# Attention, Strassen projections and a Winograd convolution on one core: softmax sums of eight heads in the first batch, stores on SP's queue, two prepared weight parts moved, and a transform ahead of outputs

## The chip, the cores and the metric

The kernel runs on one core of a Trainium2 chip. The core has a matrix engine (TensorE, PE in the profile, with its weight loads as PEld), a vector engine (VectorE, DVE), a scalar engine (ScalarE, ACT), GpSimd (POOL) and SyncE (SP). Each executes its own instructions in order and waits on semaphores for the others. SP and POOL also issue DMAs: a DMA instruction stands in its engine's order like any other, so one that waits holds back what is queued behind it. The metric is the device time of one execution in microseconds (us); the median of four runs is given. The profile is one more execution.

## What is computed

`x` is (4, 1024, 32, 32). Layer 0 is attention over the 1024 positions of each image: with 1024 channels as 16 heads of 64,

```
qkv = x @ w_qkv.T + b_qkv
q, k = rmsnorm(rope(q)), rmsnorm(rope(k))
attn = softmax(q @ k.T * 64**-0.5)
out  = rmsnorm((attn @ v) @ w_proj.T) + x
```

Layer 1 is a bottleneck block: 1x1 convolution to 256 channels, 3x3 convolution, 1x1 convolution back to 1024, each with a batch norm over the whole batch; ReLU after the first two, and after the residual sum at the end. All is float32.

## The kernel before

**Stages.** The four images ("batches" b = 0 to 3) go one after the other through the projections of q, k and v, attention, and the output projection y. Then come conv1, conv2 and conv3, all of them with activations that stay on the core or are read back from HBM.

**Projections.** Each 1024 x 1024 product is a Strassen-Winograd product (7 products of half-size blocks in place of 8). `project` does one level; it is used for q and k of batch 0. `project2` (L459) does two levels, 49 products. Sums of weight blocks are prepared once, in batch 0, and kept in HBM: `wd` holds first-level sums, `wd2` second-level ones. `prepare` (L385) makes the four sums of one outer part: four loads of 256 KB, four DVE operations of 128 x 512 (`make`, L391), four stores of 256 KB into `wd2` (L397). `prepare_blocks` (L401) does the same for `wd`. In both the stores are issued by POOL. Weight tiles come from a ring of eight buffers (`wring`), and the pieces that are prepared during attention use the same ring.

**The order of the work** is written by hand for PE, POOL, DVE and ACT: each runs its instructions in the order of the Python calls. SP's order is left to the framework. Within the projections a step can be put off by a number of products (`after(n, step)`); one product is some 3.43 us of PE time. `weight_parts` (L1122) queues loads on POOL at a given product and `make` some products later. Rotations of q and k (`turn`, L717) are queued items, run as a budget of DVE time allows.

**Attention.** `attention` (L767) runs for two halves (c = 0, 1) of the queries; each half has eight head pairs. This document counts them 0 to 15 through a batch. For a pair, 16 score products (L787, each shown as two instructions) go through ACT's exponential (L794) into eight tiles `p`; DVE adds the eight tiles into `den` (L798, L800); PE multiplies `p` with v (L808). The eight `p` tiles have no second copy. The sum of `den` over its 128 partitions is a PE product with a matrix of ones. It is done in one of two ways:

- *By pairs* (L837 to L843, `fold` is None): after every odd pair, PE sums the `den` tiles of two pairs at once, four products that show as eight instructions `dn` (L841). `inverses` (L885) then copies the result, stores it in `dens`, loads it back over all partitions, and two steps later DVE takes the reciprocal (L899), and `spread` (L905) loads it back to both halves of a tile by eight loads on SP for each two pairs.
- *By eights* (`fold` is two tiles of `T0` and `T2`): `halve` (L848) adds a pair's lower and upper 64 partitions with accumulating DMAs on POOL, so that two pairs share one tile. After four pairs, and two pairs late, `sum_of_eight` (L857) sums all four with four products (L861, eight instructions), and one pair after that the reciprocal (L868) and 16 `spread` loads follow.

Either way `mean_of_v` (L761), after odd pairs, multiplies the result by the spread reciprocals (DVE L764, POOL L765). Before the change only c = 0 of batches 1 to 3 goes by eights. In batch 0 attention also prepares 21 weight parts (`todo`, L1204): `load_parts` (L1210) loads at most two ahead with SP, and `make` runs after the pairs, one or two at a time, all done by pair 14.

**conv2** is a Winograd convolution. For each batch four items (f, h) follow each other, 2 x 2 of 128 output channels and row halves. An item's products are `uv` (L1418): a first half, then ACT copies both PSUM banks out (`copies`, L1432, into the ring `tmp` of four tiles, two for an item), then a second half into the same banks. `outputs` (L1442) combines banks and copies on DVE (L1445, L1446, and more when h is 1). It runs for the item before the current one. `steps` holds the next batch's input transform, 16 DVE operations (L1357), four of which run after each item's outputs. The last four write the tile `V` that the next batch's first item reads.

The order of one item, L1501 to L1518:

```python
uv(b, f, h, 0, 1)
copies(b, f, h)
...
for i in range(NPT):
    uv(b, f, h, 1, i)
if due:
    outputs(*due)
due = (b, f, h)
for step in steps[:4]:
    step()
steps = steps[4:]
```

Of the kernel before, what the change touches and what calls it, by code (L numbers as in the profile page):

```python
# [18 lines left out]
P = 128  # L19
# [66 lines left out]
def program(ctx, tc, x, wblk, w2, w3, vecs, cos, sin, out, bad):  # L86
# [71 lines left out]
    with tc.tile_pool(name=f"st{u}", bufs=2) as st, ExitStack() as s:  # L158
# [226 lines left out]
        def prepare(which, base, k, alloc, queue):  # L385
# [15 lines left out]
        def prepare_blocks(base, g, alloc, queue):  # L401
# [6 lines left out]
            def make():  # L408
# [4 lines left out]
                for o, t in enumerate((a11, a22, a21, a12)):  # L413
                    nc.gpsimd.dma_start(wd[base // NT * NG + g, o], t)
# [707 lines left out]
        def weight_parts(parts, first, step, lag, alloc):  # L1122

            for i, part in enumerate(parts):
                after(first + i * step, lambda part=part: after(lag, part(alloc, nc.gpsimd)))

        def pieces_of(tile, cols=NCH):
# [3 lines left out]
            def alloc(name):  # L1131
# [8 lines left out]
                lambda alloc, queue, which=which, base=base, k=k: prepare(which, base, k, alloc, queue)  # L1140
# [5 lines left out]
        def blocks_of(base):  # L1146
            return [lambda alloc, queue, g=g: prepare_blocks(base, g, alloc, queue) for g in range(NG)]
# [16 lines left out]
        for b in range(B):  # L1164
# [8 lines left out]
            if b == 0:  # L1173
                unused = kp.tile([P, NT, N], F32, tag="k", name="unused")
                parts = [
                    lambda alloc, queue, g=g: prepare_blocks(WV, g, stay(room, g), queue) for g in range(NG)
                ]
# [9 lines left out]
            if b == 0:  # L1187
# [3 lines left out]
                weight_parts([parts_of[WQ][0]], 14, 0, 4, pieces_of(room[:, : NT // 2, :]))  # L1191
# [301 lines left out]
        for b in range(B):  # L1493
# [8 lines left out]
            for f in range(NPT):  # L1502
                for h in range(2):
# [153 lines left out]
```

## Time and profile before

| | us |
|---|---|
| median of 4 runs (lowest, highest) | 2673.92 (2672.91, 2675.62) |
| the profiled execution, its own time | 2674.97 |
| span of its trace | 2672.7 |
| PE busy | 2644.0 (99%) |
| DVE busy | 2112.4 (79%) |
| ACT busy | 1111.9 (42%) |
| POOL busy | 472.2 (18%) |
| batch 0: k projection, from, to | 104.7, 201.7 |
| batch 0: attention, from, to | 287.7, 522.2 |
| batch 1: q projection, from, to | 609.7, 696.3 |
| conv2, from, to | 2432.4, 2547.0 |

The stages are read from the first and last PE instruction of their tiles; times of places count from the start of the span. In rows of the timeline the columns are: start, duration of the merged group, engine, line, operation, tiles written and read, shapes, count, and in brackets the idle time before the group and what ended it. The granted TensorE clock is at full speed through all 40 slices of the profile.

### The profile page before, as it was taken

The numbers are of one execution on the slowest core, as the hardware profiler recorded it, in microseconds if no ns is written. First come the engines' busy times: TensorE is split into PE (matmuls) and PEld (weight loads), VectorE is DVE, ScalarE is ACT, GpSimd is POOL, SyncE is SP. The second block draws the span as 40 slices with busy tenths as digits, with TensorE's granted clock in tenths as the row PEclk, the third lists the DMA queues.
The fourth block names the chain that finished last, engine by engine and source line by source line (L and its number), as shares of the span: only waits on it lengthen the run. The fifth ranks groups of instructions, "written<-read, shape, count | busy, mean of one in ns | idle before, by whom it ended". The sixth has DMA issues, their size and how long they took to land. (4 is left out here: it accounts for less than half of the span.)

```text
span 2672.7 us, 32558 instructions
## 1 busy us (share of the span) xinstructions
PE 2644.0 (99%) x11338; PEld 1651.0 (62%) x11338; DVE 2112.4 (79%) x2538; ACT 1111.9 (42%) x1549; POOL 472.2 (18%) x573
## 2 busy tenths in 40 slices
PE   9999999999999999999999999999999999999997
PEld 4448533488888333688886333888884335846843
DVE  5678899988787866788878667887988679877987
ACT  2222455423442655433343655233425654312266
POOL 2542234301001221200111222100111222010000
PEclk9999999999999999999999999999999999999999
DMA  7887676767567451456775531665774443583165
GB/s 272 292 257 216 198 243 207 234 210 247 170 182 213 81 103 46 154 152 223 190 194 148 95 74 36 209 202 178 192 213 87 83 99 112 172 278 106 64 235 207
DMA packets 255627, 459.22 MB, mean 172 GB/s; under 512 B 34912, under 2 KB 127632, under 8 KB 255456
## 3 DMA queue, kind: packets, MB, share of 16 engines
q1 hardware_dynamic: 210528, 306.73, 36.5%
q0 software_dynamic: 44928, 150.33, 22.3%
q8 instruction: 93, 1.52, 0.2%
q14 instruction: 78, 0.64, 0.1%
HBM read 327.43 MB, written 97.01 MB: 159 GB/s over the span
## 5 line engine op out<-in xcount | busy, mean ns | idle before, releaser
L794 ACT ACTIVATE p<-sc 128x1024 f32<-128x1024 f32 x512 | 476.3, 1043 | 26.4 <-PE sc L787 24.8
L787 PE MATMUL sc<-q,k 64*128 64x512 f32 x2048 | 457.7, 596 | 0.0
L800 DVE TENSOR_TENSOR den<-den,p 128x1024 f32<-128x1024 f32 x312 | 384.9, 1234 | 33.6 <-DVE den L800 1.4
L787 PEld LDWEIGHTS sc<-q,k 64*128 64x128 f32 x2048 | 189.9, 186 | 265.2 <-issue 121.6
L808 PE MATMUL cx<-p,to 128*64 128x512 f32 x1536 | 340.2, 595 | 0.0
L808 PEld LDWEIGHTS cx<-p,to 128*64 128x64 f32 x1536 | 106.0, 137 | 228.7 <-issue 228.7
L480 PE MATMUL p_v<-w_v,x 128*128 128x256 f32 x928 | 210.0, 379 | 2.1 <-DVE x L451 2.1
L485 PE MATMUL p_y<-q,w_y 128*128 128x256 f32 x928 | 209.8, 379 | 0.0
L765 POOL TENSOR_SCALAR q<-q,vec 128x512 f32<-128x512 f32 x64 | 129.0, 2023 | 384.5 <-DVE q L764 376.3
L480 PEld LDWEIGHTS p_v<-w_v,x 128*128 128x128 f32 x928 | 176.1, 190 | 27.4 <-DVE x L451 3.1
L485 PEld LDWEIGHTS p_y<-q,w_y 128*128 128x128 f32 x928 | 176.0, 190 | 27.1 <-issue 3.4
L813 ACT COPY q<-cx 128x512 f32<-128x512 f32 x64 | 37.6, 587 | 360.0 <-PE cx L808 360.0
L798 DVE TENSOR_TENSOR den<-p 128x1024 f32<-128x1024 f32 x52 | 64.7, 1243 | 120.3 <-ACT p L794 120.3
L485 PE MATMUL p_q<-to,w_q 128*128 128x256 f32 x672 | 152.2, 379 | 0.0
L485 PE MATMUL p_k<-to,w_k 128*128 128x256 f32 x672 | 152.2, 379 | 0.0
L485 PEld LDWEIGHTS p_q<-to,w_q 128*128 128x128 f32 x672 | 127.4, 190 | 18.4 <-issue 1.2
L485 PEld LDWEIGHTS p_k<-to,w_k 128*128 128x128 f32 x672 | 127.4, 190 | 18.4 <-issue 1.2
L808 PE MATMUL cx<-p,rq 128*64 128x512 f32 x512 | 113.4, 595 | 0.0
L1561 PE MATMUL c<-h,w 128*128 128x512 f32 x256 | 110.3, 592 | 0.5 <-ACT h L1464 0.5
L800 DVE TENSOR_TENSOR den_T<-den_T,p 128x1024 f32<-128x1024 f32 x72 | 88.2, 1225 | 7.5
L485 PE MATMUL p_y<-to,w_y 128*128 128x256 f32 x384 | 90.4, 380 | 1.7 <-DMA w_y<-wdf 1.7
L727 POOL DMA_DIRECT2D k<-ks x64 | 57.9, 1096 | 192.8 <-ACT p L794 71.1
(490 smaller groups left out, 4267.8 us busy)
## 6 DMA issues: line engine op xcount, KB each, us to landing
w_v<-wd2f SPq DMA_DIRECT2D x112, 256.0 KB, 3.5
w_y<-wd2f SPq DMA_DIRECT2D x112, 256.0 KB, 2.7
w_q<-wd2f SPq DMA_DIRECT2D x84, 256.0 KB, 2.8
w_k<-wd2f SPq DMA_DIRECT2D x84, 256.0 KB, 2.7
wd2f<-w_pre POOLq DMA_DIRECT2D x68, 256.0 KB, 4.0
x<-in_x_dram SPq DMA_DIRECT2D x64, 256.0 KB, 5.7
q<-qs POOLq DMA_DIRECT2D x64, 256.0 KB, 5.5
k<-ks POOLq DMA_DIRECT2D x64, 256.0 KB, 4.4
```

Source lines behind the costliest of these rows:

```text
L480: nc.tensor.matmul(o[:, q].rearrange("p (g f) -> p g f", g=2), r[:, i, q * P : (q + 1) * P], wt[:, :, i, :], skip_group_check=True, **at,)
L485: nc.tensor.matmul(o[:, q], wt[:, q, i, :], r[:, i, :], skip_group_check=True, **at)
L727: nc.gpsimd.dma_start(dst[i::2, f, :], other[1 - i :: 2, :], accum_op=ALU.add)
L765: nc.gpsimd.tensor_scalar(cx, cx, col("bv", hp), None, ALU.add)
L787: nc.tensor.matmul(sc[:, j], k_all[d, hp, t * P : (t + 1) * P], q_all[d, hp, at], start=True, stop=bad is not None,)
L794: nc.scalar.activation(p, sc, AF.Exp)
L798: nc.vector.tensor_tensor(d_, probs[0], p, ALU.add)
L800: nc.vector.tensor_tensor(d_, d_, p, ALU.add)
L808: nc.tensor.matmul(o[j * HD : (j + 1) * HD, :], v[:, t, h0 : h0 + HD], probs[t][:, j], start=(t == 0), stop=(t == N // P - 1),)
L813: nc.scalar.copy(q_all[:, hp, at], o)
L1561: nc.tensor.matmul(os[i], w3t[k][f // NH][:, f % NH, :], h2[b, k][:, half[c]], start=(k == 0), stop=(k == NPT - 1),)
```

## The change

It has four parts.

1. `fold[0]` is made for batch 0 too, so the first half of its queries goes by eights.
2. `prepare` and `prepare_blocks` take the engine that stores as an argument. The parts prepared during batch 0's attention are now stored from SP; those that `weight_parts` handles stay on POOL.
3. Two items move. `WQ` part 1 leaves attention's list and is prepared in batch 0's k projection, with part 0, which is made earlier there (load at product 4.5 and not 14, `make` 3.5 later; part 1 four products after it). `WK` part 5 leaves batch 1's q projection and goes to the end of attention's list, which keeps 21 items.
4. In conv2, after the last item of a batch, the four transform operations run ahead of `outputs` and not after it.

The diff, cut to its core:

```diff
-        def prepare(which, base, k, alloc, queue):
+        def prepare(which, base, k, alloc, queue, back):
...
-                    nc.gpsimd.dma_start(wd2[which, k, m], t)
+                    back.dma_start(wd2[which, k, m], t)
...
-        def prepare_blocks(base, g, alloc, queue):
+        def prepare_blocks(base, g, alloc, queue, back):
...
-                    nc.gpsimd.dma_start(wd[base // NT * NG + g, o], t)
+                    back.dma_start(wd[base // NT * NG + g, o], t)
...
-                after(first + i * step, lambda part=part: after(lag, part(alloc, nc.gpsimd)))
+                after(first + i * step, lambda part=part: after(lag, part(alloc, nc.gpsimd, nc.gpsimd)))
...
-            elif b == 1:
-                weight_parts([parts_of[WK][5]], 9, 0, 4, pieces_of(room[:, : NT // 2, :]))
...
-                weight_parts([parts_of[WQ][0]], 14, 0, 4, pieces_of(room[:, : NT // 2, :]))
+                for k, at in ((0, 0), (1, NT // 2)):
+                    weight_parts([parts_of[WQ][k]], 4.5 + 4 * k, 0, 3.5, pieces_of(room[:, at : at + 2, :]))
...
-                todo += [parts_of[WQ][k] for k in (1, 3, 4, 5)] + [parts_of[WK][k] for k in (0, 1, 6, 2, 3, 4)]
+                todo += [parts_of[WQ][k] for k in (3, 4, 5)] + [parts_of[WK][k] for k in (0, 1, 6, 2, 3, 4, 5)]
...
-                    made.append(todo.pop(0)(pieces, nc.sync))
+                    made.append(todo.pop(0)(pieces, nc.sync, nc.sync))
...
-            fold = [None, None]
-            if b > 0:
-
-                fold[0] = [tp.tile([P, NH, CH], F32, tag=t, name=f"den_{b}_{t}") for t in ("T0", "T2")]
+
+            fold = [[tp.tile([P, NH, CH], F32, tag=t, name=f"den_{b}_{t}") for t in ("T0", "T2")], None]
...
+
+                    last = (f, h) == (NPT - 1, 1)
+                    for step in steps[:4] if last else []:
+                        step()
                     if due:
                         outputs(*due)
                     due = (b, f, h)
-                    for step in steps[:4]:
+                    for step in [] if last else steps[:4]:
                         step()
```

More of the change, by code (lines that the diff above doesn't have):

```diff
@@ L1139, in program @@
             base: [
-                lambda alloc, queue, which=which, base=base, k=k: prepare(which, base, k, alloc, queue)
+                lambda *how, which=which, base=base, k=k: prepare(which, base, k, *how)
                 for k in range(len(OUTER))
@@ L1146, in blocks_of @@
         def blocks_of(base):
-            return [lambda alloc, queue, g=g: prepare_blocks(base, g, alloc, queue) for g in range(NG)]
+            return [lambda *how, g=g: prepare_blocks(base, g, *how) for g in range(NG)]
         vector_and_act = {mybir.EngineType.DVE, mybir.EngineType.Activation}
@@ L1175, in program @@
                 parts = [
-                    lambda alloc, queue, g=g: prepare_blocks(WV, g, stay(room, g), queue) for g in range(NG)
+                    lambda alloc, *queues, g=g: prepare_blocks(WV, g, stay(room, g), *queues) for g in range(NG)
                 ]
                 weight_parts(parts + [parts_of[WV][k] for k in (0, 1, 6)], 8, 2.4, 4, pieces_of(unused))
-            elif b == 1:
-                weight_parts([parts_of[WK][5]], 9, 0, 4, pieces_of(room[:, : NT // 2, :]))
             tq = qk_proj(b, WQ, xs[b], ts[b], "bq", q_all, "q", w1 if b == 0 else None, two, True)
```

## The prediction

> **What bounds the kernel.** I read the page first. PE is busy nearly the whole span at full clock, so time leaves only with PE work or with a PE wait.
>
> ```profile
> PE   9999999999999999999999999999999999999997
> PEclk9999999999999999999999999999999999999999
> ```
>
> [...]
>
> In attention each pair takes 7.07 us of scores and 7.02 of products with v, start after start; in batch 0, pair 1 begins at 301.86 and its second half at 308.93. That cadence has no hole.
>
> Then I read who PE waited for. These are all the waits PE has; they say what can be won beyond dropped work.
>
> ```profile
> PE pa_q L303 <- DMA x<-in_x_dram: 5.9, 1, 5.9
> PE p_v L480 <- DVE x L451: 2.1, 2, 1.2
> PE p_y L485 <- DMA w_y<-wdf: 1.7, 2, 1.5
> PE c2x L1422 <- DVE V L1357: 1.5, 2, 1.0
> PE p_q L485 <- DMA w_q<-wdf: 1.1, 1, 1.1
> PE p_y L485 <- DVE rec L891: 0.7, 1, 0.7
> ```
>
> Columns: us in total, times, longest. The change can reach the last four, 5.0 us together.
>
> **Part 1, eights in batch 0.** The sums are in PE's timeline, by pairs at batch 0's pair 1, and by eights in batch 1:
>
> ```profile
> 315.94 2.17 PE L841 MATMUL dn<-den,ones 128*32 128x512 f32 x8
> 318.05 4.13 PE L787 MATMUL sc<-q,k 64*128 64x512 f32 x18
> ...
> 946.01 1.06 PE L861 MATMUL dn<-den_T,halves 128*32 128x512 f32 x8
> 947.01 7.09 PE L808 MATMUL cx<-p,to 128*64 128x512 f32 x32
> ```
>
> Start to next start, a group costs 1.00 us (946.01 to 947.01). Four by pairs become two by eights: -2.0. The first took 2.11 (315.94 to 318.05), 1.1 over: PE waited for DVE's last `den` of pair 1, which ends at 317.0. By eights nothing reads that `den` for two pairs: -1.1. **Together -3.1.**
>
> What could take it back is DVE, busy 214.1 of the 234.5 us of this attention (windows by stage). Its rows: the `den` chain of a pair 9.2 us, starting at best 3.15 after the pair's first score; a `make` 2.75; a `mean_of_v` product 0.61. At best it ends 12.35 after the first score, and the second half of the pair ends at 14.09, so in pairs 9, 11, 13, 15, still summed by pairs, DVE may be 1.75 late before PE pays. Eights gather four `mean_of_v` at pairs 7 and 11. Walking the pairs with these rows, DVE is 0.9 late at pair 9 if those four find their rows landed; a wait w there costs PE about w - 0.9.
>
> The rows: in this attention eight `spread` loads took SP 390.36 to 394.33, so sixteen take 8.0; the store before them 1.4 (388.92 to 390.36); the last lands 2.3 to 5.3 after its issue. That is 11.7 to 14.7 after the reciprocal; DVE comes back for the second two means 15.0 after it (a pair of 14.09 and two means, less what stands between). With four part stores and four loads between them on SP, 0.33 to 0.5 each, up to 4 more. So w is -3 to 4. I take 1.5 at one place: **+0.6**, from 0 to +5 (w = 4 at both places, where the walk gives 3.1 and 2). `halve` on POOL delays nobody: in batch 1 its last DMA for pair 7 lands at 995.0, and PE reads at 1003.4. Batch 0 has DVE some 3 us later, so 5 are left.
>
> **Part 2, stores on SP.** 84 stores leave POOL (0.54 us each) for SP (0.33 for a plain load of that size). Neither is on PE's path. What is queued behind a store that waits for DVE's `make` is the next pieces' load, the `few` loads and `spread`. But that load waits today for the same store to land, since the ring has eight buffers: SP stood from 288.14 to 316.4 for it. So the wait is not new: **0**. Bounds: DVE's 0.78 us wait for `few` at 506.18 goes (-0.8), or SP holds `few` one landing longer, 4.0 us for such a store, less the 1.75 of slack (+2.3).
>
> [...]
>
> After attention PE waits twice in the y projection, at 528.40 for the last reciprocal and at 543.94 for weights queued on SP behind that reciprocal's eight loads, 0.7 and 1.5 us. PE and DVE both arrive some 3 us earlier, DVE a little more: **-0.3**, from -2.2 to +1.
>
> **Part 3, WK part 5 leaves batch 1's q projection.** Its four POOL loads are issued 641.0 to 643.9 and land by 651.5, beside weights that SP issues at 645.15; PE then waits 1.1 at 654.81. The q projections of batches 2 and 3, which lack these loads, have no such wait. **-1.1**, from -1.2 to 0 (the stores of `y`, 512 KB each, stay). At attention's end the part replaces one of equal kind; 21 items remain.
>
> **WQ parts 0 and 1 in batch 0's k projection.** DVE works there without a gap from 126.3 to 157.9. Part 0's `make` moves from 170.04 to about 134; part 1's is new, near 152. Four operations of 0.69 each. The next sums, for weights 1b and 2b, are these:
>
> ```profile
> 146.92 0.69 DVE L238 TENSOR_TENSOR w_k_1b<-w_k_1b_s,w_k_1b 128x512 f32<-128x512 f32 x1
> ...
> 160.61 1.22 DVE L723 TENSOR_TENSOR qs<-q,sinT 128x1024 f32<-128x1024 f32 x1 [2.62 <-DMA q<-qs]
> ...
> 164.45 0.69 DVE L238 TENSOR_TENSOR w_k_2b<-w_k_2b_s,w_k_2b 128x512 f32<-128x512 f32 x1
> ```
>
> PE reads 1b at 150.12 and 2b at 167.28. 1b would be ready at 147.61 + 2.75 = 150.36, 0.3 late. 2b is pushed by both, 5.5, less up to 2.62 of idle time that DVE spends waiting for a rotation's DMA: 165.14 + 2.9 to 5.5 = 168.0 to 170.6, that is 0.4 to 3.0 late after the 0.3. For 3b (DVE waits 5.7 for its load before 182.40) traffic is lighter once part 0 is gone. **+1.2**, nearest to the lower end since the rotations shift with DVE; from 0 to +3.3. Were that idle time not there, the upper end would be the value.
>
> **Part 4, conv2.** Three views meet at the step from batch 0 to 1: DVE, then PE, then ACT.
>
> ```profile
> 2461.43 0.68 DVE L1445 TENSOR_TENSOR n<-c2x,c2y 128x512 f32<-128x512 f32 x1
> 2462.03 0.68 DVE L1446 TENSOR_TENSOR n<-c2x,c2y 128x512 f32<-128x512 f32 x1
> 2462.62 4.63 DVE L1357 TENSOR_TENSOR V<-cols 128x1024 f32<-128x1024 f32 x4
> ```
>
> ```profile
> 2463.90 0.70 PE L1422 MATMUL c2x<-V,t_w 128*128 128x256 f32 x2 [1.02 <-DVE V L1357]
> 2465.03 0.70 PE L1422 MATMUL c2x<-V,t_w 128*128 128x256 f32 x2 [0.44 <-DVE V L1357]
> ...
> 2466.43 1.11 PE L1422 MATMUL c2x<-V,t_w 128*128 128x256 f32 x4
> ```
>
> ```profile
> 2465.77 0.59 ACT L1437 COPY c2x<-c2x 128x512 f32<-128x512 f32 x1 [2.97 <-PE c2x L1422]
> ```
>
> With the transform first, V begins 1.19 earlier and the two waits shrink from 1.5 to some 0.4: -1.1. But `n` (L1445, L1446) reads the copies of item (0,1,0), and `tmp` has four tiles, two for an item: the copy of (1,0,0) writes the tile that L1446 reads. The two `n` would now end at 2461.43 + 4.55 + 1.25 = 2467.2, not 2462.6; the ACT copy goes there from 2465.77, and PE, which needs the bank copied, from 2466.43 to about 2468.0: **+1.6** net. At the next boundary the second `n` would end near 2494.6 against a copy at 2493.72 + 1.6: no further wait, and none at the third. Ends: -1.1 if the copy does not wait, +2.5 if the second boundary also pays its 0.9.
>
> **Sum.** -3.1 + 0.6 + 0 - 0.3 - 1.1 + 1.2 + 1.6 = **-1.1**. The profiled execution's own time is 2674.97, its span 2672.7, with 2.3 outside that nothing here touches; it would become 2673.9. It lies 1.05 above the median, so against the median of 2673.92 I say **2672.8**. About 0.2%, 5.3 us, is what a measurement of this kernel can tell from no change.
>
> **Rivals.**
>
> *The gains stay whole* (0.15). DVE in the k projection absorbs its operations, and the copy in conv2 does not wait on `n`. For it: the 2.62 of idle time in the one, the absence of any such ACT wait today in the other. Against it: four tiles, two per item. -3.1 - 0.3 - 1.1 + 0 - 1.1 = -5.6: 2668.3.
>
> *Late rows* (0.13), the slower side. At pairs 7 and 11 of batch 0 DVE stands in `mean_of_v` for the 16 loads that queue on SP among part stores and loads; pairs 9 and 13 pay. It decides from w = 0.9. For it: 217 GB/s in this stage against 73 in batch 1's attention, where eights run freely, and landings up to 5.3. Against it: in all of today's batch 0 DVE waits for such rows only 0.2 us. At w = 5 it pays 4.1 + 3.0, and the y projection 0.5 in place of -0.3: -3.1 + 7.1 + 0.5 - 1.1 + 1.2 + 1.6 = +6.2: 2680.1.
>
> *Eights bring nothing in batch 0* (0.12). DVE is the real pace there, so PE's 3.1 turn into waits at pairs 9 to 15 and in y. For it: 91% DVE. Against it: DVE catches up with ACT at pairs 2, 4, 6, 7 and 14. 0 - 1.1 + 1.2 + 1.6 = +1.7: 2675.6.
>
> The forecast has 0.60. Range 2668 to 2679.5: the low end is the first rival, the high end late rows at a little under w = 5. Beyond 0.2% lie about half of the first rival and some of the forecast's own spread, 0.10 faster; half of the second and the K projection at its upper end, 0.09 slower; 0.81 within.
>
> **What the changed profile would show.** No L841 in batch 0 before pair 9, and its pair 1 lasting 14.1, not 16.2. L764 waiting at pairs 7 and 11, or not. PE without a wait near 655. DVE L238 ending after PE's due time twice in the k projection. In conv2 ACT's copy released by DVE's `n`. I am wrong if batch 0's attention does not shrink by 2 to 3.1, or if conv2 gets shorter.

## Result and profile after

| | before | after |
|---|---|---|
| median, us (lowest to highest, executions) | 2673.89 (2670.63 to 2679.44, 52) | 2677.31 (2670.29 to 2682.56, 32) |
| after over before, 95% interval | | 1.0013 (1.0008 to 1.0018) |
| profiled execution, its own time; its span | 2674.97; 2672.7 | 2682.23; 2680.4 |
| k projection, batch 0 | 97.15 | 103.04 |
| v projection, batch 0 | 85.79 | 86.83 |
| attention, batch 0 | 234.54 | 234.56 |
| y projection, batch 0 | 87.45 | 87.07 |
| q projection, batch 1 | 86.70 | 85.37 |
| conv2 | 114.29 | 117.09 |

The change made the kernel slower by 3.4 us in the median (2.1 to 4.8 by the interval). The forecast was 1.1 us faster. A stage here lasts from its first PE instruction to the first of the next stage. The profiled execution of after is at the high end of its kernel's executions, 4.9 above their median, so the table overstates: the stages shown differ by +8.0 us, the two spans by +7.8. The v and y projections vary by themselves: conv_only (below), which changes nothing there, has 86.39 and 86.98.

Who PE waited for, in us in total, times, and the longest, after:

```profile
PE pa_k L303 <- DVE w_k_3b L238: 3.3, 1, 3.3
PE c2x L1419 <- ACT c2x L1434: 2.0, 1, 2.0
...
PE dn L841 <- DVE den L800: 0.6, 2, 0.3
...
PE c2x L1419 <- DVE V L1354: 0.4, 1, 0.4
PE pa_k L303 <- DVE w_k_1b L238: 0.2, 1, 0.2
PE pa_k L303 <- DVE w_k_2b L238: 0.2, 1, 0.2
```

The wait near 655 for `w_q` (1.1) is gone, and the one for `V` shrank from 1.5 to 0.4. New are 3.3 for weight 3b in the k projection and 2.0 for ACT's copy in conv2. The small ones for 1b and 2b were forecast.

**k projection.** The timeline of after, POOL, SP's queue, DVE and PE (columns as before):

```profile
172.96 1.73 POOL L727 DMA_DIRECT2D q<-qs  x2 [2.07 <-DVE q L723]
176.33 1.70 POOL L727 DMA_DIRECT2D q<-qs  x2 [1.64 <-DVE q L723]
177.27 0.33 SPq L226 DMA_DIRECT2D w_k_3b<-in_wblk_dram  x1
177.52 1.66 POOL L176 DMA_DIRECT2D sinT<-in_sin_dram  x2
...
186.88 0.69 DVE L236 TENSOR_TENSOR w_k_3b_s<-w_k_3b,w_k_3b 128x512 f32<-128x512 f32 x1 [9.45 <-DMA w_k_3b<-in_wblk_dram]
...
182.17 3.60 PE L303 MATMUL pa_k<-t,w_k_2b 128*128 128x512 f32 x8
189.08 5.40 PE L303 MATMUL pa_k<-t,w_k_3b 128*128 128x512 f32 x8 [3.31 <-DVE w_k_3b L238]
```

The last load of 3b takes 9.6 us from issue to DVE's start. Before the change it took 6.1 (176.26 to 182.40), and four stores of a part (`wd2f<-rq`, 174.18 to 177.27) stood on POOL between the swaps (`q<-qs`, transfers of the rotation that add into q). POOL and DVE of before:

```profile
172.32 0.86 POOL L727 DMA_DIRECT2D q<-qs  x1 [0.39 <-DMA q<-qs]
174.18 0.60 POOL L397 DMA_DIRECT2D wd2f<-rq  x1 [1.00 <-DVE qs L723]
...
177.93 1.74 POOL L727 DMA_DIRECT2D q<-qs  x2
...
182.40 0.69 DVE L236 TENSOR_TENSOR w_k_3b_s<-w_k_3b,w_k_3b 128x512 f32<-128x512 f32 x1 [5.70 <-DMA w_k_3b<-in_wblk_dram]
```

Then PE of after does eight products in 5.40 us, where the eight ahead of the wait take 3.60. The windows view shows why; its PE clock is the third column from the end:

```profile
185.40:189.00 3.60, 0.37 (x1) 0.00 (x0) 2.05 (x3) 1.32 (x2) 0.00 (x0) 1.00 0.88 325
189.00:193.50 4.50, 4.42 (x7) 1.88 (x8) 3.88 (x7) 1.26 (x2) 2.16 (x4) 0.62 0.67 249
189.40:192.80 3.40, 3.40 (x5) 1.35 (x4) 3.29 (x6) 1.26 (x2) 2.08 (x4) 0.50 0.69 253
193.50:197.00 3.50, 3.50 (x10) 1.59 (x9) 0.00 (x0) 0.59 (x1) 0.00 (x0) 1.00 0.28 81
```

Over the 4.5 us after the wait the mean granted clock was 0.62, from 189.4 to 192.8 it was 0.50. That cost another 1.8 us.

**conv2.** DVE, ACT and PE of after at the step from batch 0 to 1:

```profile
2470.99 0.69 DVE L1442 TENSOR_TENSOR n<-c2x,c2y 128x512 f32<-128x512 f32 x1
2471.59 0.68 DVE L1443 TENSOR_TENSOR n<-c2x,c2y 128x512 f32<-128x512 f32 x1
2471.77 0.59 ACT L1434 COPY c2x<-c2x 128x512 f32<-128x512 f32 x1 [4.07 <-DVE n L1442]
2472.41 1.62 PE L1419 MATMUL c2x<-V,t_w 128*128 128x256 f32 x4 [1.98 <-ACT c2x L1434]
```

The copy waits for DVE's `n`, as the prediction had it. By its bracket it waits for the first of the two (L1442); the second (L1443), which the prediction reckoned with, is still running when the copy starts. Four products then take 1.62 us where 1.11 was usual: a low clock again (a mean of 0.62 from 2472.4 to 2476.9).

**Attention of batch 0.** DVE, POOL and PE of after around pairs 7 to 9:

```profile
406.85 2.90 DVE L764 TENSOR_TENSOR q<-q,inv 128x512 f32<-128x512 f32 x4
409.67 0.68 DVE L392 TENSOR_TENSOR w_pre<-w_pre,w_pre 128x512 f32<-128x512 f32 x1
410.39 1.06 DVE L393 TENSOR_TENSOR w_pre<-w_pre,w_pre 128x512 f32<-128x512 f32 x1
...
412.21 1.07 DVE L395 TENSOR_TENSOR w_pre<-w_pre,w_pre 128x512 f32<-128x512 f32 x1
...
416.34 1.22 DVE L798 TENSOR_TENSOR den<-p 128x1024 f32<-128x1024 f32 x1
...
427.08 0.69 DVE L392 TENSOR_TENSOR w_pre<-w_pre,w_pre 128x512 f32<-128x512 f32 x1 [1.55 <-DMA w_pre<-wdf]
...
407.64 7.67 POOL L765 TENSOR_SCALAR q<-q,vec 128x512 f32<-128x512 f32 x4 [13.69 <-DVE q L764]
...
439.12 1.05 PE L841 MATMUL dn<-den,ones 128*32 128x512 f32 x4 [0.24 <-DVE den L800]
```

L764 has no wait in brackets: the rows were there. But while POOL adds the bias four times, operations of a `make` take 1.06 in place of 0.69 us, and a later `make` waits 1.55 for its load. In all, 7 of the 84 `make` operations are so lengthened. Before the change it was 12, beside two additions at a time:

```profile
345.97 4.18 POOL L765 TENSOR_SCALAR q<-q,vec 128x512 f32<-128x512 f32 x2 [7.18 <-DVE q L764]
348.76 1.06 DVE L395 TENSOR_TENSOR w_pre<-w_pre,w_pre 128x512 f32<-128x512 f32 x1
```

In after DVE starts the `den` chain of pair 8 4.5 us later than the 3.15 after the first score that it manages at best. The time from one pair's first score to the next one's, in us (pair 15: to the y projection):

| pair | 1 | 3 | 7 | 9 | 13 | 15 |
|---|---|---|---|---|---|---|
| before | 16.19 | 15.08 | 15.08 | 15.08 | 15.08 | 15.08 |
| after | 14.08 | 14.09 | 14.09 | 17.36 | 15.54 | 16.45 |

Pair 9 holds two sums now, so 16.08 is due there. The gain of 3.1 is all there by pair 9, and 1.3 + 0.5 + 1.4 at pairs 9, 13 and 15 take it back.

### The profile page after: what moved, and what is told of

It reads as the page before. It is cut to its first block, busy times and chain, and to the rows that moved or that the text cites. A ratio compares the mean times of both kernels' runs of the same rounds, so it can differ in the third digit from the quotient of the medians.

```text
span 2680.4 us, 32428 instructions
## 1 busy us (share of the span) xinstructions
PE 2648.0 (99%) x11322; PEld 1652.9 (62%) x11322; DVE 2112.5 (79%) x2536; ACT 1111.0 (41%) x1547; POOL 433.8 (16%) x501
## 5 line engine op out<-in xcount | busy, mean ns | idle before, releaser
L800 DVE TENSOR_TENSOR den<-den,p 128x1024 f32<-128x1024 f32 x288 | 355.8, 1235 | 30.7 <-DVE den L798 0.5
L800 DVE TENSOR_TENSOR den_T<-den_T,p 128x1024 f32<-128x1024 f32 x96 | 117.6, 1225 | 10.0
L480 PE MATMUL p_v<-w_v,t 128*128 128x256 f32 x384 | 90.1, 379 | 0.8 <-DMA w_v<-wdf 0.8
```

Of the source, the lines that this page charges most:

```text
L480: nc.tensor.matmul(o[:, q].rearrange("p (g f) -> p g f", g=2), r[:, i, q * P : (q + 1) * P], wt[:, :, i, :], skip_group_check=True, **at,)
L800: nc.vector.tensor_tensor(d_, d_, p, ALU.add)
```

## Experiments

The median is that of the kernel's own executions (4 to 11), the ratio is to those of the kernel before on the same chip, whose medians were 2672.86 to 2674.08. Medians that differ by 2 us are hardly told apart this way, so verdicts rest on the stages of the profiles. Where an expectation named a gain in the median over after, it mostly did not come: by the ratios u_items is 0.8 us below after (expected 3 to 6), u_conv2 0 (2.8), tables_late 1.9 (3 to 5.5) and wq1_late 1.3 (2 to 5); conv_split has 2.1 (2 to 3). Each of these differences is uncertain by some 2.8 us, an estimate from the two intervals.

| kernel | median | ratio (95%) | k, batch 0 | attention, batch 0 | conv2 |
|---|---|---|---|---|---|
| u_items | 2676.08 | 1.0010 (1.0001 to 1.0019) | 97.27 | 232.72 | 117.07 |
| tables_late | 2676.58 | 1.0006 (0.9997 to 1.0015) | 99.87 | 237.92 | 115.39 |
| wq1_late | 2676.28 | 1.0008 (0.9999 to 1.0017) | 98.99 | 236.07 | 117.09 |
| u_conv2 | 2677.82 | 1.0013 (1.0004 to 1.0022) | 103.33 | 233.62 | 114.28 |
| conv_split | 2675.96 | 1.0005 (0.9996 to 1.0014) | 99.72 | 235.24 | 113.22 |
| u_eights | 2680.69 | 1.0030 (1.0018 to 1.0042) | 104.19 | 234.54 | 117.07 |
| u_stores | 2691.36 | 1.0070 (1.0056 to 1.0084) | 102.46 | 244.39 | 115.38 |
| smooth | 2685.92 | 1.0038 (1.0024 to 1.0051) | 102.28 | 240.06 | 117.08 |
| later | 2681.16 | 1.0026 (1.0014 to 1.0037) | 102.31 | 238.51 | 115.40 |
| no_make_dve | 2724.48 | 1.0196 (1.0180 to 1.0212) | 102.54 | 280.16 | 115.39 |
| no_bias_pool | 2676.03 | 1.0010 (1.0000 to 1.0019) | 101.91 | 231.44 | 115.39 |
| best1 | 2673.78 | 1.0003 (0.9994 to 1.0012) | 99.34 | 234.11 | 113.23 |
| best2 | 2673.35 | 0.9999 (0.9990 to 1.0008) | 97.02 | 233.97 | 113.23 |
| conv_only | 2671.65 | 0.9993 (0.9984 to 1.0002) | 97.20 | 234.54 | 113.23 |
| q1_alone | 2672.12 | 1.0000 (0.9991 to 1.0009) | 97.18 | 236.70 | 113.22 |
| bias_act | 2671.82 | 0.9994 (0.9985 to 1.0003) | 97.22 | 231.45 | 113.21 |

### The k projection

**u_items**: the change with the two items in their old places.

```diff
+            elif b == 1:
+                weight_parts([parts_of[WK][5]], 9, 0, 4, pieces_of(room[:, : NT // 2, :]))
...
-                for k, at in ((0, 0), (1, NT // 2)):
-                    weight_parts([parts_of[WQ][k]], 4.5 + 4 * k, 0, 3.5, pieces_of(room[:, at : at + 2, :]))
+                weight_parts([parts_of[WQ][0]], 14, 0, 4, pieces_of(room[:, : NT // 2, :]))
...
-                todo += [parts_of[WQ][k] for k in (3, 4, 5)] + [parts_of[WK][k] for k in (0, 1, 6, 2, 3, 4, 5)]
+                todo += [parts_of[WQ][k] for k in (1, 3, 4, 5)] + [parts_of[WK][k] for k in (0, 1, 6, 2, 3, 4)]
```

> The changed kernel with the two moved items put back (WQ part 0 late in batch 0's k projection, WQ part 1 in attention's list, WK part 5 in batch 1's q projection). Theory: the moved items are the largest loss. The k projection of batch 0 falls from 103.0 to 97.2 to 97.5 us, the v projection by up to 1.0, while batch 1's q projection rises from 85.4 to 86.7; net 3 to 6 us below the changed kernel. Rival: the late weight tile 3b is a chance of one execution, the k projection in the changed kernel is usually near 98, and putting the items back changes the time by less than 1 us.

The k projection is back at 97.27, the q projection of batch 1 at 86.98. Both effects belong to the items, in the profile; the median does not show the 3 to 6 us. In the timeline the load of 3b took 6.3 us (issue 175.48):

```profile
181.82 0.69 DVE L236 TENSOR_TENSOR w_k_3b_s<-w_k_3b,w_k_3b 128x512 f32<-128x512 f32 x1 [5.89 <-DMA w_k_3b<-in_wblk_dram]
```

**tables_late**: my first theory was the reload of the rope tables, which in after is issued beside that load.

```diff
-                    load_tables(nc.gpsimd)
-                    pace["tables"] = pace["at"] + 3.7
+                    if (b, tag) == (0, "q"):
+                        after(3, lambda: load_tables(nc.gpsimd))
+                        pace["tables"] = pace["at"] + 6.7
+                    else:
...
```

> One edit to the changed kernel: in the first batch the reload of the rope tables behind the q projection is put off by three products, so that its three transfers are issued after w_k_3b's last load and not together with it. Theory (the moved part took its stores away from POOL's queue, so the tables start 2 to 3 us earlier and share the DMA engines with w_k_3b's last load, which then lands 9.5 us after its issue instead of 5.9 to 6.2): that load lands in 6 to 7 us again, TensorE's wait for w_k_3b of 3.3 us falls to at most 0.6, the low granted clock behind it is gone, and the k projection of the first batch takes 97.3 to 98.5 us instead of 103.0; the median falls by 3 to 5.5 us against the changed kernel, and its runs lie closer together. Rival (the ring slot that the load needs comes free late, because the stores of w_k_2b land late, whatever the tables do): the wait stays above 2 us and the projection at 101 us or more, median unchanged within 1 us. A third (the later tables make the k rope late): the projection is short and the v projection or the first batch's attention is longer by as much.

The tables came at 189.0, well after, and the load still took 8.6 us (issue 175.75; the DVE row gives its end). PE waited 1.85:

```profile
184.34 0.69 DVE L236 TENSOR_TENSOR w_k_3b_s<-w_k_3b,w_k_3b 128x512 f32<-128x512 f32 x1 [8.37 <-DMA w_k_3b<-in_wblk_dram]
...
186.54 3.70 PE L303 MATMUL pa_k<-t,w_k_3b 128*128 128x512 f32 x8 [1.85 <-DVE w_k_3b L238]
```

The shorter wait proves nothing: conv_split, with the tables where after has them, shows 7.8 us and a wait of 1.4. The tables theory falls as the cause. That late tables help a little is not excluded: with them the load takes 8.6 us here and 7.6 in best1, in the nine kernels with after's tables 7.8 to 9.8.

**wq1_late**: part 1 starts where part 0 stood before the change, so its stores are among the rope's swaps (`q<-qs`, L727, which accumulate into q) again.

```diff
-                    weight_parts([parts_of[WQ][k]], 4.5 + 4 * k, 0, 3.5, pieces_of(room[:, at : at + 2, :]))
+                    weight_parts([parts_of[WQ][k]], 4.5 + 9.5 * k, 0, 3.5 + k / 2, pieces_of(room[:, at : at + 2, :]))
```

> One edit to the changed kernel: in the first batch's k projection the second of the two moved parts (WQ part 1) starts at product 14 and not at 8.5, so that its four stores on POOL's queue fall between the rope's q swaps at 174 to 177 us, where part 0's stood before the change. The swaps accumulate in memory, one lands 1.6 to 2.3 us after the other; the stores land 0.7 to 0.9 us apart. Theory (w_k_3b's last load on SP's queue is served in turn with what POOL's queue holds; without the stores that is four swaps in a row, and the load takes 7.6 to 9.5 us; with the stores between them it takes 5.9 to 6.2 again): the load lands within 6.5 us, TensorE's wait for w_k_3b is at most 0.6 us, k projection 97.2 to 98.3 us, median 2 to 5 us below the changed kernel. Rival (the transfers simply have more to move since two parts are handled here instead of one, so a later part only adds to it): the load takes 8 us or more and the projection 99.5 or more. A third (part 1 at that place is late for its buffer, which the v projection writes): the projection is short, the v projection longer by a microsecond or more.

```profile
174.36 0.86 POOL L727 DMA_DIRECT2D q<-qs  x1 [0.52 <-DMA q<-qs]
176.40 0.60 POOL L397 DMA_DIRECT2D wd2f<-rq  x1 [1.18 <-DVE qs L723]
177.23 1.17 POOL L397 DMA_DIRECT2D wd2f<-rq  x2 [0.24 <-DMA q<-qs]
179.04 0.54 POOL L397 DMA_DIRECT2D wd2f<-rq  x1 [0.64 <-DMA wdf<-w_k_2b]
...
184.46 0.69 DVE L236 TENSOR_TENSOR w_k_3b_s<-w_k_3b,w_k_3b 128x512 f32<-128x512 f32 x1 [5.83 <-DMA w_k_3b<-in_wblk_dram]
...
186.66 3.70 PE L303 MATMUL pa_k<-t,w_k_3b 128*128 128x512 f32 x8 [1.39 <-DVE w_k_3b L238]
```

With four stores between the swaps the load takes 6.8 us (issue 177.71), with more traffic than in after (335 GB/s while it runs, against 265). Over all profiles: with stores there 5.9 to 6.8 (eight profiles: before, u_items, best2, conv_only, q1_alone, wq1_late and the two of bias_act), without them 7.6 to 9.8 (eleven). The stores land 0.7 to 1.3 us apart, the swaps in after 1.8 to 2.5, and the load ends with the last of four swaps (186.56 and 186.76 in after). In all 19 profiles DVE starts on 3b within 0.4 us of the seventh landing on POOL's queue after the load's issue. The first five are three stores of 2b's sums and two swaps; the last two are either stores, which take 1.8 to 2.2 us together, or swaps, which take 3.3 to 4.9. The theory's tie between the load's time and the transfers beside it holds; that queues are served in turn is not shown. The stage was to be 97.2 to 98.3 and is 99.0, since the load is also issued later. From the stage's start that is 71.5 us before the change, 72.3 after, 72.8 here: the buffer that it needs is freed by the first store of 2b's sums (in all three kernels it lands 0.14 us before the issue), and these sums come later because of the moved `make`s (they begin 61.1 us from the stage's start in after, 60.0 in wq1_late, 58.3 before).

The packets of POOL's queue (q0) while the load runs, in after (177.3 to 186.8) and in wq1_late (177.7 to 184.4), with their number, MB and share of the 16 engines:

```profile
q0 software_dynamic: 603, 2.00, 87.5%
q0 software_dynamic: 548, 1.80, 87.0%
```

That is a mean of 0.22 us for a packet in after and 0.17 in wq1_late (an estimate: the share, times 16 engines, times 9.5 and 6.7 us, over the number): beside the slower packets the load took 9.6 us, beside the others 6.8. In what order an engine takes them, no view here shows.

### conv2

**u_conv2** puts the order back; **conv_split** runs two of the four transform operations ahead of `outputs` and two behind.

```diff
-                    last = (f, h) == (NPT - 1, 1)
-                    for step in steps[:4] if last else []:
-                        step()
...
-                    for step in [] if last else steps[:4]:
+                    for step in steps[:4]:
```

```diff
-                    for step in steps[:4] if last else []:
+                    for step in steps[:2] if last else []:
...
-                    for step in [] if last else steps[:4]:
+                    for step in steps[2:4] if last else steps[:4]:
```

> The changed kernel with conv2's order put back: outputs ahead of the transform everywhere. Theory: the transform ahead of outputs made ACT's copy of item (1,0,0) wait for DVE's second n, PE stood 2.0 us and then ran its products at twice their spacing. So conv2 falls from 117.1 to 114.3 us, the ACT wait on n disappears, the two short waits on V (1.5 us together) come back, and the time is some 2.8 us below the changed kernel. Rival: the order in conv2 is worth nothing (DVE has the same work), conv2 stays within 0.5 us and the whole loss lies elsewhere.

> One edit to the changed kernel: in the second convolution only two of the last four transform operations go ahead of the outputs, the other two follow them. Theory (the four operations push DVE's second n behind the time at which ScalarE's copy of c2x is due, the copy holds TensorE's first product of the next bank by 2.0 us, and the clock granted afterwards falls to 0.61 for some 4.4 us): with half of them behind, the copy waits 1.9 us less, TensorE's wait is at most 0.5 us, the low clock is gone, and the convolution takes 113.5 to 114.4 us instead of 117.1; median 2 to 3 us below the changed kernel. Rival (it is the transform's last operations that the next products need, so whatever goes behind the outputs is waited for at V): the wait at V comes back at 1.0 to 1.5 us and the convolution stays above 115.

114.28 and 113.22: the one as its theory says, the other a little better (113.5 to 114.4). The split keeps the gain at `V` without the wait for the copy. PE of conv_split at the place of the old wait:

```profile
2465.85 0.70 PE L1419 MATMUL c2x<-V,t_w 128*128 128x256 f32 x2 [0.44 <-DVE V L1354]
2466.39 1.03 PE L1419 MATMUL c2y<-V,t_w 128*128 128x256 f32 x4
2467.25 1.11 PE L1419 MATMUL c2x<-V,t_w 128*128 128x256 f32 x4
```

Ten kernels keep the changed order. All have the wait of 1.98; five take 117.1 and five 115.4. This is tables_late:

```profile
2471.39 1.13 PE L1423 MATMUL c2x<-V,t_w 128*128 128x256 f32 x4 [1.98 <-ACT c2x L1438]
```

Same wait, full clock afterwards. So the order costs 1.1 and the low clock, when it comes, 1.7 more.

### The first attention

**u_eights** sums batch 0 by pairs again; **u_stores** keeps the eights and stores from POOL.

```diff
-            fold = [[tp.tile([P, NH, CH], F32, tag=t, name=f"den_{b}_{t}") for t in ("T0", "T2")], None]
+            fold = [None, None]
+            if b > 0:
+                fold[0] = [tp.tile([P, NH, CH], F32, tag=t, name=f"den_{b}_{t}") for t in ("T0", "T2")]
```

```diff
-                    made.append(todo.pop(0)(pieces, nc.sync, nc.sync))
+                    made.append(todo.pop(0)(pieces, nc.sync, nc.gpsimd))
```

> The changed kernel with batch 0 summed by pairs again; the stores stay on SP, the items and conv2 as changed. Theory: eights save PE 3.1 us up to pair 8 and DVE gives them back at pairs 9, 13 and 15, so batch 0's attention stays at 234.5 within 1 us, with its pair 1 at 16.2 again and pair 9 back from 17.4 to 15.1; the time stays within 1 us of the changed kernel. Rival: eights alone cost, and the stores gain: attention falls by 2 us or more. Other rival: eights gain their 3.1, and the stores cost them: attention rises to about 237.

> The changed kernel with the stores of attention's weight parts back on POOL; all else as changed. Theory: DVE's wait of 1.55 us for a part's load at pair 9 comes from loads that queue on SP behind eight stores; but on POOL the same stores queue behind four tensor operations of 2 us at pairs 7, 11 and 13, so the loads come later still: attention 234.5 to 238, the time 0 to 3 us above the changed kernel. Rival: SP is what holds the loads up; with POOL's queue the waits go and attention falls to 232.5.

By pairs 234.54, the same as before and as the whole change: the stores on SP cost and bring nothing by themselves. With eights and stores on POOL it is 244.39, far beyond what I expected. POOL of u_stores, and a DVE row:

```profile
407.04 7.66 POOL L765 TENSOR_SCALAR q<-q,vec 128x512 f32<-128x512 f32 x4 [8.06 <-DVE q L764]
...
418.43 4.63 POOL L397 DMA_DIRECT2D wd2f<-w_pre  x8
...
431.83 0.69 DVE L392 TENSOR_TENSOR w_pre<-w_pre,w_pre 128x512 f32<-128x512 f32 x1 [6.89 <-DMA w_pre<-wdf]
```

The stores stand behind the four additions and the two transfers of `halve`, the next loads behind the stores, and a `make` waits 6.89 us. Given eights, SP is worth 6.5 to 10.8 us: the six kernels whose attention is after's, unchanged (after, tables_late, wq1_late, u_conv2, conv_split, best1), take 233.6 to 237.9.

**smooth** moves one `make` from pair 7 to 6 and one from 9 to 10; **later** moves them from 7 to 8 and from 9 to 10.

```diff
+                move = {6: -1, 9: 1}.get(c * NHP + hp, 0)
-                for _ in range(len(extra) - -(-steps_in_all * max(slots - 1 - c * NHP - hp, 0) // slots) if steps_in_all else 0):
+                for _ in range(len(extra) - move - -(-steps_in_all * max(slots - 1 - c * NHP - hp, 0) // slots) if steps_in_all else 0):
```

(later: `move = int(c * NHP + hp in (7, 9))`.)

> One edit to the changed kernel: in the first batch's attention one weight part's make moves from the end of pair 7 to that of pair 6, and one from pair 9 to pair 10. Theory (the eights' four means and two makes meet at pair 7, DVE is 4.5 us late at pair 8, and TensorE waits for its sums at pair 9, which takes back the gain of pairs 1, 3 and 7): pair 9 takes 15.1 to 16.1 us instead of 17.4, the first batch's attention 232.7 to 233.4 instead of 234.6, median down by 0.8 to 2. Rival (the loads of the parts queue on SP behind the eight stores, and the make waits for them wherever it stands): the wait moves to pairs 7 or 11 and the attention stays at 234 to 236 us.

> One edit to the changed kernel: in the first batch's attention one of two makes goes from pair 7 to pair 8 and one from pair 9 to pair 10 (the run before it had moved one the other way, to pair 6, where its load was late). Theory (four means and two makes in one pair are what makes DVE late): with one make beside the four means, DVE starts pair 8 about 1.0 to 1.5 us late instead of 4.5, no make waits over 1 us for its load, pair 9 takes 15.1 to 16.3 instead of 17.4, and the attention 232.5 to 233.8 us instead of 234.6. Rival (loads: SP's queue holds eight stores ahead of the next loads wherever two makes meet, and then the make waits): a wait of 1.5 us or more for w_pre appears at pair 9, 10 or 11, and the attention stays at 234.3 or above.

Both are worse, as their rivals have it, smooth by more than its rival said. In smooth a `make` waits 3.5 us for its load at pair 7 and another 2.7 at pair 11. In later, pairs 8 and 9 are as wished (DVE 1.4 late, pair 9 takes 16.08), but a `make` waits 1.9 us for its load at pair 11 and the next reciprocal 1.8 for its rows, and pair 13 takes 20.1.

**no_make_dve** leaves DVE's operations out of the parts made here; **no_bias_pool** leaves out POOL's additions in batch 0.

```diff
-                nc.vector.tensor_tensor(a22, a21, a22, ALU.add)
...
+                if back is not nc.sync:
+                    nc.vector.tensor_tensor(a22, a21, a22, ALU.add)
...
```

```diff
-            nc.gpsimd.tensor_scalar(cx, cx, col("bv", hp), None, ALU.add)
+            if bias:
+                nc.gpsimd.tensor_scalar(cx, cx, col("bv", hp), None, ALU.add)
```

> The changed kernel without DVE's four operations in each of the 21 parts that are made in the first batch's attention; their loads and stores stay (the weights so stored are not the sums that they should be). Theory (DVE's time at the pairs with four means and two makes takes back the gain): the attention takes 231.4 to 231.9 us as in the later batches, where no parts are made, 2.7 to 3.1 us less than the 234.6 of the changed kernel. Rival (the loads, stores and the traffic of the parts hold DVE's sums or the rows of the reciprocals): it stays at 233.5 or above, with waits of DVE or TensorE for DMA.

> The changed kernel without POOL's bias additions behind the means in the first batch's attention (the bias is left out of those heads). Theory (POOL's four additions of 1.9 us in a row lengthen DVE's L393 and L395 from 0.69 to 1.06 us beside them and so make half of the lateness at pair 8): these operations take 0.69 us, DVE starts pair 8 some 1.5 us less late, and the attention takes 233 to 234 us. Rival (the lengthening comes from something else, DMA traffic say): the two operations stay at 1.06 us. A third (they shorten, but the next loads are then what is waited for): 0.69 us, and the attention still above 234.

no_make_dve tells nothing of its question. Without those operations the framework orders SP's queue otherwise: the first store of a sum comes behind the parts of all later pairs, at 446.33, and DVE stands 60.30 us for its rows. no_bias_pool is clear on one point: all `make` operations take 0.69 us, and the attention 231.44, the level of the later batches. The lateness at pair 8 hardly moved (4.3), since a load was 1.17 late there.

**bias_act** keeps the additions but gives them to ScalarE, on top of best2 (below).

```diff
+            if act:
+                biases.append(lambda: nc.scalar.activation(cx, cx, AF.Identity, bias=col("bv", hp)))
+            else:
...
+                add_biases()
                 nc.scalar.copy(q_all[:, hp, at], o)
```

> The kernel of eights, stores on SP and the split convolution order (moved items in their old places), and in the first batch's attention the bias behind the means is added by ScalarE, one pair later, ahead of its copy of cx where it waits for TensorE some 6 us per pair. Theory (POOL's additions beside DVE's two-input operations make DVE late): L393 and L395 behind the means take 0.69 us and not 1.06, pair 13 takes 15.1 us, the attention 231.4 to 232.8 us, k projection 97.2, convolution 113.2, median 2669.5 to 2671.5, below the kernel before by 0.1 to 0.15%. Rival (the late load of a part at pair 8 is what matters, not POOL): pair 9 takes 16.4 to 18 us in the profile, the attention 233.3 or more, the median 2672.5 to 2674. A third (ScalarE's additions delay its exponentials): periods of even pairs above 14.1.

> One more look at the kernel of the run before, for its stage times alone: the same as there if the load at pair 8 is not what varies; pair 9 longer or shorter by 1 to 3 us if it is.

The second expectation is for a second profile of this same kernel (one execution, 2675.39). DVE behind the means at pair 7, first profile:

```profile
400.22 2.49 DVE L770 TENSOR_TENSOR q<-q,inv 128x512 f32<-128x512 f32 x4
402.63 0.68 DVE L392 TENSOR_TENSOR w_pre<-w_pre,w_pre 128x512 f32<-128x512 f32 x1
403.35 0.69 DVE L393 TENSOR_TENSOR w_pre<-w_pre,w_pre 128x512 f32<-128x512 f32 x1
...
405.47 0.69 DVE L392 TENSOR_TENSOR w_pre<-w_pre,w_pre 128x512 f32<-128x512 f32 x1
```

DVE is 3.1 late at pair 8, pairs 9 and 13 take 16.08 and 15.08, the attention 231.45. The second profile of the same kernel, same place:

```profile
408.25 0.69 DVE L392 TENSOR_TENSOR w_pre<-w_pre,w_pre 128x512 f32<-128x512 f32 x1 [3.50 <-DMA w_pre<-wdf]
```

One load 3.5 us late: 6.6 late at pair 8, pair 9 takes 17.78, the attention 234.30. So both causes are real, and they add: 3.1 + 1.5 of POOL is the 4.5 of after, 3.1 + 3.5 of a late load is this 6.6. The load's part differs between these two executions of one program. The six kernels with after's attention differ by 4.3 us for the same reason: at pair 9 their `make` waits 0.5 to 3.4 us for its load, and the longer that wait, the longer the pair, 16.3 to 20.1. What pairs 13 and 15 lose (0.4 to 1.1 and 1.4 in the six) is gone in the first profile of bias_act. The gain is also lost elsewhere: v projection of batch 2, 89.7 and 89.5 in these two profiles (86.2 in after), with a wait for `x` of 2.3 and 2.1 and a low clock behind it (a mean of 0.84 and 0.85 over 11 us). Why `x` is late there is not shown.

### Which parts are worth keeping

**best1** is tables_late and conv_split together; **best2** is u_items with conv_split's order; **conv_only** is the kernel before with that order alone; **q1_alone** is conv_only with `WK` part 5 moved out of the q projection into attention:

```diff
-            elif b == 1:
-                weight_parts([parts_of[WK][5]], 9, 0, 4, pieces_of(room[:, : NT // 2, :]))
...
-                ... + [parts_of[WK][k] for k in (0, 1, 6, 2, 3, 4)]
+                ... + [parts_of[WK][k] for k in (0, 1, 6, 2, 3, 4, 5)]
```

> The two edits of the runs before it together: rope tables put off by three products, two transform operations instead of four ahead of the outputs. Theory (the two delays are independent, 600 products apart): k projection of the first batch 97.3 to 98.5, second convolution 113.5 to 114.4, and a median of 2669 to 2671.5, faster than the kernel before the change by 0.1 to 0.2%. Rival (the profiles' stage times overstate, since not every execution has these waits): the median is 2672 to 2674, the same as before the change.

> The kernel before with the parts of the change that kept their gain: sums of eight heads in the first batch, stores on SP, and two of the last four transform operations ahead of the outputs in the second convolution; the moved items are back in their old places. Theory (the eights are worth 1.8 us in the first batch's attention when DVE has no more to do there, and the split order 1.1 us in the convolution): first attention 232.4 to 233.0, second convolution 113.2, k projection 97.2, median 2670.5 to 2672.5, below the kernel before by 0.05 to 0.13%. Rival (the eights' gain is not in every execution, since their loads and sums meet in time at pairs 7 to 9, and the runs scatter as the changed kernel's do): median 2673 to 2676.

> The kernel before the change with one edit: two of the last four transform operations ahead of the outputs in the second convolution. Theory: the convolution takes 113.2 us instead of 114.3, all else as before, median 0.8 to 1.3 us below the kernel before. Against the run of eights with this order it prices the eights alone: 1.8 us more if they keep their gain, nothing or less if they don't. Rival: the gain of the convolution is given back where the transform's last blocks are stored, and the median is the same.

> The kernel before with the split order of the second convolution, and with WK part 5 taken out of the second batch's q projection and added to the parts made in the first attention (22 instead of 21, by pairs, stores on POOL); nothing is moved into the k projection. Theory: the q projection of the second batch takes 85.4 instead of 86.2 to 86.7, the convolution 113.2, the k projection stays at 97.2, and the attention grows by less than 1 us: median 2670 to 2671.5, below the kernel before by 0.08 to 0.15%. Rival (one more make delays DVE's sums at an odd pair): the attention takes 235.5 us or more and the gain is gone.

best1 gains nothing over the kernel before; its first attention and k projection are still 234.1 and 99.3. In best2 the eights bring 0.6 us in the profile and nothing in the median. q1_alone shortens the q projection to 85.37 and pays 2.2 us in attention for the 22nd part. conv_only is the one part with a gain in its stage (113.23 for 114.29) and nothing to pay; its interval, 0.9984 to 1.0002, and that of bias_act, 0.9985 to 1.0003, still take in 1. No version here is shown to beat the kernel before.

## Why the prediction was wrong

It said 1.1 us faster; the median moved by +3.4. One of its own signs of being wrong came up too: the attention of batch 0 was to shrink by 2 to 3.1 us and is 234.56 for 234.54. The step that failed first is the one on the WQ parts, "For 3b (DVE waits 5.7 for its load before 182.40) traffic is lighter once part 0 is gone. +1.2".

- **WQ parts, +1.2 (0 to +3.3).** Measured +2.6 to +7.0 in nine profiles with this stage unchanged from after (99.7 to 104.2, median 102.5, against 97.2). 1b and 2b came 0.2 to 0.5 late, at the lower end, as forecast. At 3b I counted bytes and not whose transfers they are. The four stores that left had stood between the rope's accumulating swaps. Without them the load of 3b runs beside four swaps and takes 7.6 to 9.8 us in place of 6.1, and it is issued 0.7 later. That it is the swaps is shown by wq1_late, and by the seventh landing in all profiles; in what way they slow it, no view here shows.
- **conv2, +1.6 (-1.1 to +2.5).** The mechanism is right: V's waits shrink by 1.1, ACT's copy waits for `n`, PE for the copy. Its size without the low clock is +1.1, since the copy waits for the first `n` and I had reckoned with the second, 0.6 later. The term left out is the clock, +1.7 in half of the profiles.
- **Eights, -3.1.** Right row by row: pair 1 is 2.1 shorter, the sums net 1.0; bias_act shows the whole -3.1.
- **DVE gives back, +0.6 (0 to +5).** Measured 3.1 in after (2.2 to 6.5 in the six kernels with its attention); 1.3 and 2.5 with the items back (u_items and best2), all against 231.45. The place is right (means and `make`s at pair 7, paid at 9 and 13, and also at 15), the reason not: no wait for rows. I priced a `make` at 2.75 beside anything; next to POOL's additions it takes 3.5, as the trace of before showed (12 operations there are lengthened, 348.76 is one), and I took the parts' loads as always early.
- **Stores on SP, 0.** By pairs 0, as u_eights shows. With eights they are what makes the eights possible at all; I had not asked what a store on POOL meets when four means come together.
- **q projection, -1.1: -1.33.** Right; it is 85.37 in every kernel with the item moved. **y projection, -0.3: -0.38.** The number fits, but y varies by more without the change (86.98 in conv_only, 87.45 before), so this shows nothing.
- The rivals: late rows did not occur, the gains did not stay whole. "Eights bring nothing", 2675.6, is the nearest, for another reason than it gave.
- Unsettled: how much of the median's +3.4 is the WQ parts. Their stage is 2.6 to 7.0 longer in each of the nine profiles, but taking both items back lowers the median by 0.8 (u_items), which is uncertain by 2.8. Also, u_eights is slower than the whole change in the medians (intervals 1.0018 to 1.0042 and 1.0008 to 1.0018), though its attention lasts as long in the profiles; and the executions of after, 2670.3 to 2682.6, scatter more than those of before. A load that is late in one execution of a program (3.50 us) and not in another is shown by bias_act, and the clock after the same wait of 1.98 us by ten kernels; both fit, but no profile shows a fast execution of after.

## What to carry to other kernels

When a transfer is moved, ask not only what it met in its new place but what stood around it in the old one: it may have kept slower transfers of its queue apart, or held them back (here the load beside them took 9.6 us in place of 6.1). Waits of PE of 1.98 to 3.74 us cost another 1.5 to 3.0 us in clock here in 13 of 18 cases, eight at 3b and five of ten in conv2, so price that too. A gain that is handed to an engine at 91% (DVE: 214.1 of 234.5 us) is a gain only if its operations keep their length beside the others and its loads keep their time (here a `make` took 3.5 us in place of 2.75, and its loads came up to 3.5 late); take both from the worst rows of the trace, not from the usual ones.

## What the runs showed of the hardware

- **The granted clock fell after some of PE's waits.** After a wait of PE of up to 1.85 us at 3b (four kernels) the clock stayed at 1.00 (eight products in 3.70 us in tables_late and wq1_late); after 2.19 to 3.74 us (eight kernels) the stage lost another 1.5 to 3.0 us. Five of these eight have the row: the eight products took 5.18 us (later), 5.40 (after, no_make_dve, no_bias_pool) and 6.72 (u_eights). In the other three (u_conv2, u_stores, smooth) the stage is 1.9 to 2.1 us longer than 97.15 and its waits give, against 0.2 to 0.5 in the four; that this is the clock is an estimate from the stage times. In after the products took twice their spacing, 0.85 for 0.43 us, at a clock of 0.50 over 3.4 us. After 1.98 us in conv2 the stage took 117.1 us in five kernels (in after at a clock of 0.62 over 4.5 us) and 115.4 in five (in tables_late at 1.00); what decides between them is not shown.
- **POOL's additions lengthen some of the `make` operations of DVE beside them**, from 0.69 to between 0.98 and 1.07 us for 128 x 512 (12 of 84 before, 7 in after), and take 1.9 to 2.1 us each themselves. The operations in between stay at 0.69. Without the additions (no_bias_pool), or with them on ScalarE (bias_act), all take 0.69. By what way POOL lengthens them is not shown.
- **The same store landed sooner from SP**: the page's median from issue to landing of `wd2f<-w_pre` is 2.4 us from SP in after and 4.0 from POOL before (4.0 again in u_stores), with the DMA share of this attention at 0.76 in after and 0.67 before.
